# The row of node numbers for the one-hot comparison, read from the PSUM bank of running counts

## The chip, the core and the metric

The kernel runs on one core of a Trainium2 chip. The metric is the device time of one execution in microseconds (us). Five engines work side by side, each through its own queue in order: PE (matrix products, with its weight loads as a row of their own, PEld), DVE (vector operations), ACT (activations and copies), POOL (here almost only the issue of scattered DMAs) and SP (here only DMA issue). SBUF is the working memory. PSUM is the memory that PE writes its results to, in eight banks; DVE and ACT read and write it too.

## The reference

A graph network layer over 12500 nodes with 64 features and 212500 edges that come sorted by their destination `dst`:

```python
h = relu(layernorm(x))
e = silu(concat([h[src], h[dst], edge_weight]) @ eW1 + eb1)   # 129 -> 128, per edge
e = silu(e @ eW2 + eb2)                                       # 128 -> 128, per edge
agg = segment_sum(e, src, num_segments=12500)                 # sum over edges with one source
out = x + silu(concat([h, agg]) @ nW1 + nb1) @ nW2 + nb2      # per node
```

Everything is in 32-bit floating point. The sums go by `src`, while the edges are sorted by `dst`.

## The kernel before

The nodes are dealt to 100 buckets of 125 nodes (`L = 125`, `NB = 100`). The per-node products `h @ eW1` for the source half (`ta`) and the destination half (`tb`) are computed first, a few buckets at a time, and kept in DRAM. Then two kinds of work run interleaved.

**Blocks.** The edges are read in 208 blocks of 1024 in the order given. For a block, `count` finds a row in a bucket-ordered table `q` in DRAM for each edge. DVE compares bucket numbers (`oh`, line 393) and sums them per partition (`each`, line 398). PE adds these sums to the running counts of all buckets with two matmuls onto one PSUM tile named `counts` (lines 413 and 432), which holds 128 x 100 numbers in a bank of its own. DVE reads the counts back (`mine`, line 447; `rank`, line 449) and writes the destinations `to` (line 451), of which four buffers exist. `send` then makes the `tb` part of each edge by PE matmuls (`qp`, line 475), ACT copies it to `qs` (lines 484 and 485), and POOL scatters 128 edges at a time to `q` (line 488, 1661 scatters). A block is issued in four pieces: `oh` and `each` in the first, the matmul of line 413 in the second, that of line 432 in the third, `mine`, `rank` and `to` in the fourth.

**Steps.** As soon as a rank range of `q` is full ("level", 16 of them), the rows of four buckets at a time are loaded (`qt`, line 559) and worked on in 450 steps of 512 edges. A step consists of `lr` (PE, line 596, spreads each edge's number of the node within the bucket over partitions), `oneT` (DVE, line 601), `pt` (PE, lines 610 and 616, adds the `ta` part), a silu on ACT (line 620), the product with `eW2` (line 648), a silu (line 652), `one` (DVE, line 629) and `seg` (PE, line 662). `one` is a 0/1 matrix of 128 edges x 125 nodes for each of four tiles: it is 1 where the edge's node number equals the column's number. It compares `nodes1`, a row 1 to 125 in SBUF, the same on all partitions, with the edge's number in `qt`. `seg` multiplies it with the edges' values and so sums them per node; `aggT` (DVE, line 673) adds the sums of a batch to those so far.

The order on PE, DVE, ACT and SP is written out by hand. The loop at line 1072 goes through the list `turn` (line 681) for each step: `s_pt` of the next step, `s_add`, `s_one_t` two steps ahead, `s_bias`, `s_p2`, `s_one`, `s_seg` of the step before, `s_lr` three steps ahead. At its four `None` places, which are after `s_one_t`, `s_one`, `s_seg` and `s_lr`, pieces of blocks are put in, so many that the table's levels are full when the steps need them. Semaphore waits between engines are put in by the framework from what each instruction reads and writes.

After the last scatter the remaining steps run, and the node part (`nodes`, line 279) writes the output.

Of the kernel before, what the change touches and what calls it, by code (L numbers as in the profile page):

```python
# [28 lines left out]
F32 = mybir.dt.float32  # L29
# [9 lines left out]
P = 128  # L39
L = 125  # L40
# [34 lines left out]
def tile_gnn(ctx: ExitStack, tc: tile.TileContext, x, src, dst, ew, eW1, eb1, eW2, eb2, nW1, nb1, nW2, nb2, out):  # L75
    nc = tc.nc
# [4 lines left out]
    NB = N // L  # L81
# [55 lines left out]
    nodes_i = const.tile([P, L], I32, name="nodes_i")  # L137
# [5 lines left out]
    nodes1 = const.tile([P, L], F32, name="nodes1")  # L143
# [164 lines left out]
    with ExitStack() as work:  # L308
        mm = work.enter_context(tc.tile_pool(name="mm", bufs=4, space=PSUM))
        p2p = work.enter_context(tc.tile_pool(name="p2", bufs=2, space=PSUM))  # L310
        sgp = work.enter_context(tc.tile_pool(name="sg", bufs=1, space=PSUM))
# [2 lines left out]
                engines={mybir.EngineType.PE, mybir.EngineType.DVE, mybir.EngineType.Activation, mybir.EngineType.SP}  # L314
            )
        )
        full = sgp.tile([P, NB], F32, name="counts")
        nc.tensor.matmul(full, before, identb[:, :NB], start=True, stop=True)
        nc.vector.memset(full, -1.0)
        mine = cnt.tile(twos, F32, name="mine")  # L320
        sums = []
        blk, lists = {}, {}
# [262 lines left out]
        def of(k):  # L585

            c, B, n, g = steps[k]
            return batch[c, B], [((g * G + t) % n * G + (g * G + t) // n, (g * G + t) // n) for t in range(G)]
# [34 lines left out]
        def s_one(k):  # L623
            (qt, _, _), tiles = of(k)
            c, B, n, g = steps[k]
            wide = [P, G // n, n, L]
            loc = qt[:, : G * n, H : H + 1].rearrange("p (j b) w -> p b j w", b=G)
            one = wk.tile([P, G, L], F32, name="one")
            nc.vector.tensor_tensor(  # L629
                one.rearrange("p (b j) l -> p b j l", j=n),  # L630
                nodes1[:, None, None, :].to_broadcast(wide),
                loc[:, tiles[0][1] : tiles[0][1] + G // n].to_broadcast(wide),
                op=OP.is_equal,
            )
            st[k]["one"] = one
            if g == n - 1:
                fetch(c * (NB // G) + B + NQ)
# [26 lines left out]
        def s_add(k):  # L664
# [14 lines left out]

        turn = [  # L680
            (s_pt, 1), (s_add, -2), (s_one_t, 2), None, (s_bias, 1), (s_p2, 0), (s_one, 0), None, (s_seg, -1), None, (s_lr, 3), None,
        ]
        hooks = sum(1 for s in turn if s is None)
# [559 lines left out]
```

## Time and profile before

| | |
|---|---|
| median of 3 runs | 2368.57 us (2365.8 to 2370.33) |
| profiled execution | 2374.24 us, its span 2372.4 us |
| PE busy | 2103.3 us (89%), mean granted clock 0.962 |
| DVE busy | 1857.0 us (78%) |
| ACT busy | 1180.9 us (50%) |
| POOL busy | 1697.3 us (72%) |
| scatters, line 488 | 1661, mean 1005 ns |
| `one`, line 629 | 450, mean 673 ns |

How to read the rows that follow. A group row has line, engine, operation, output `<-` inputs by the program's names, shapes and count; behind the bar stand busy time in us and the mean of one in ns, then the idle time of the engine just before these instructions with what ended most of it. A timeline row has start in us, duration in us, engine, line, operation, operands; in brackets the engine's idle time before it and what released it. A row of waits has who waited `<-` for whom, us in total, times, and the longest where a third number stands. A row of a stretch has its bounds and length, then the busy us (with the number of instructions) of PE, PEld, DVE, ACT and POOL, the granted clock, the DMA share and GB/s.

### The profile page before, as it was taken

The numbers are of one execution on the slowest core, as the hardware profiler recorded it, in microseconds if no ns is written. First come the engines' busy times: TensorE is split into PE (matmuls) and PEld (weight loads), VectorE is DVE, ScalarE is ACT, GpSimd is POOL, SyncE is SP. The second block draws the span as 40 slices with busy tenths as digits, with TensorE's granted clock in tenths as the row PEclk, the third lists the DMA queues.
The fourth block names the chain that finished last, engine by engine and source line by source line (L and its number), as shares of the span: only waits on it lengthen the run. The fifth ranks groups of instructions, "written<-read, shape, count | busy, mean of one in ns | idle before, by whom it ended". The sixth has DMA issues, their size and how long they took to land.

```text
span 2372.4 us, 49836 instructions
## 1 busy us (share of the span) xinstructions
PE 2103.3 (89%) x17399; PEld 1847.2 (78%) x17399; DVE 1857.0 (78%) x3291; ACT 1180.9 (50%) x3262; POOL 1697.3 (72%) x1711
## 2 busy tenths in 40 slices
PE   3685888789999999998999889999989999999998
PEld 2452667678888888887788778888878888889998
DVE  7985667678888888787888788878788888788665
ACT  3463554445555555554445445545455555555543
POOL 5677777777777777777777777777777777777310
PEclk9975899899999999999999999999999999999999
DMA  4475676555555555555555555555654444444564
GB/s 136 156 251 194 218 242 190 166 185 174 178 180 173 170 177 176 173 170 157 170 164 172 168 162 172 164 167 170 190 165 131 134 135 135 137 135 141 160 214 122
DMA packets 241429, 401.83 MB, mean 169 GB/s; under 512 B 47528, under 2 KB 140195, under 8 KB 240965
## 3 DMA queue, kind: packets, MB, share of 16 engines
q1 hardware_dynamic: 149411, 216.21, 30.7%
q0 software_dynamic: 53568, 123.20, 14.5%
q10 hardware_dynamic: 38192, 59.17, 8.8%
q8 instruction: 139, 2.28, 0.4%
q14 instruction: 119, 0.97, 0.1%
HBM read 191.09 MB, written 207.01 MB: 168 GB/s over the span
## 4 chain that ended last, share of the span: by engine, by line
PE 50%; DMA 22%; DVE 11%; POOL 6%; issue 6%; ACT 4%; DVEq 0%; SPq 0%; ACTq 0%; POOLq 0%
DMA q<-qs,to 16%; PE seg L662 11%; PE pt L616 10%; PE p L648 8%; POOL q L488 6%; PE qp L475 6%; DMA qt<-q 6%; PE pt L610 6%; PE lr L596 3%; DVE aggT L673 2%; DVE each L398 1%; PE ab L215 1%; ACT e L620 1%; PE z L286 1%; PE o L295 1%
## 5 line engine op out<-in xcount | busy, mean ns | idle before, releaser
L488 POOL DMA_INDIRECT q<-qs,to x1661 | 1669.2, 1005 | 542.5 <-issue 306.1
L620 ACT ACTIVATE e<-pt 128x512 f32<-128x512 f32 x450 | 268.9, 597 | 765.5 <-PE pt L616 704.3
L662 PE MATMUL seg<-one,e 128*128 128x125 f32 x3600 | 505.0, 284 | 106.1 <-DVE aggT L673 89.4
L662 PEld LDWEIGHTS seg<-one,e 128*128 128x128 f32 x3600 | 445.9, 195 | 144.3 <-DVE aggT L673 72.8
L648 PE MATMUL p<-w,e 128*128 128x128 f32 x3600 | 486.1, 278 | 0.0
L648 PEld LDWEIGHTS p<-w,e 128*128 128x128 f32 x3600 | 441.9, 192 | 12.5 <-issue 10.5
L484 ACT COPY qs<-qp 128x256 f32<-128x256 f32 x831 | 309.2, 372 | 266.6 <-PE qp L475 261.4
L601 DVE TENSOR_SCALAR oneT<-lr,part 125x512 f32<-125x512 f32 x450 | 335.1, 745 | 19.2 <-PE lr L596 12.8
L673 DVE TENSOR_TENSOR aggT<-aggT,seg 128x500 f32<-128x500 f32 x425 | 284.4, 669 | 64.6 <-PE seg L662 61.2
L475 PE MATMUL qp<-win,pick 64*128 64x256 f32 x1662 | 319.3, 452 | 17.0 <-ACT qs L484 5.9
L629 DVE TENSOR_TENSOR one<-nodes,qt 128x500 f32<-128x500 f32 x450 | 302.7, 673 | 0.0
L610 PE MATMUL pt<-ident,qt 128*128 128x128 f32 x1800 | 286.1, 283 | 1.4 <-ACT zn L267 0.9
L652 ACT ACTIVATE e<-p 128x512 f32<-128x512 f32 x450 | 269.6, 599 | 30.2 <-PE p L648 18.9
L642 ACT COPY p<-b2f 128x512 f32<-128x512 f32 x450 | 267.6, 595 | 0.0
L616 PE MATMUL pt<-oneT,al 125*128 125x128 f32 x1952 | 262.2, 278 | 0.0
L451 DVE SCALAR_TENSOR_TENSOR to<-rank,offE 128x8 int32<-128x8 f32 x208 | 36.6, 176 | 286.7 <-DMA q<-qs,to 282.1
L616 PEld LDWEIGHTS pt<-oneT,al 125*128 125x128 f32 x1952 | 242.2, 195 | 0.0
L447 DVE TENSOR_TENSOR mine<-oh,counts 128x800 f32<-128x800 bf16 x208 | 204.0, 981 | 39.8 <-PE counts L432 39.5
L596 PE MATMUL lr<-identb,qt 128*125 128x128 bf16 x1800 | 186.9, 228 | 49.6 <-DMA qt<-q 49.1
L610 PEld LDWEIGHTS pt<-ident,qt 128*128 128x128 f32 x1800 | 196.5, 145 | 27.2 <-issue 22.9
L596 PEld LDWEIGHTS <-qt 128*125 128x125 bf16 x1800 | 156.9, 141 | 76.3 <-DMA qt<-q 63.7
L449 DVE TENSOR_REDUCE rank<-mine 128x8 f32<-128x800 f32 x208 | 205.1, 986 | 7.2
(176 smaller groups left out, 1945.7 us busy)
## 6 DMA issues: line engine op xcount, KB each, us to landing
qt<-q SPq DMA_DIRECT2D x450, 288.0 KB
q<-zeros ACTq DMA_DIRECT2D x70, 720.0 KB
q<-qs,to POOLq DMA_INDIRECT x1661
bc<-dests SPq DMA_DIRECT2D x103, 128.0 KB
win<-tb SPq DMA_DIRECT2D x416, 30.0 KB
tb<-got SPq DMA_DIRECT2D x25, 256.0 KB
zd<-zn SPq DMA_DIRECT2D x25, 250.0 KB
zh<-zd SPq DMA_DIRECT2D x25, 250.0 KB
```

The lines of the kernel that those rows point to most:

```text
L475: nc.tensor.matmul(qps[i_][:, :m], pick[half, t * P : (t + 1) * P], win[half, :m], start=True, stop=True)
L484: nc.scalar.copy(qs[:, :m, :H], qp[:, :m, :])
L488: ins = nc.gpsimd.indirect_dma_start(out=q[:], out_offset=bass.IndirectOffsetOnAxis(ap=to[:k, j : j + 1], axis=0), in_=qs[:k, a, :], in_of ...
L596: nc.tensor.matmul(lr[:L, t, :], loc[:, at : at + 1].to_broadcast([P, L]), identb, start=True, stop=True)
L601: nc.vector.tensor_scalar(oneT, st[k].pop("lr")[:L], part1[:L, :], None, op0=OP.is_equal)
L610: nc.tensor.matmul(pt[:, t, :], qt[:, j, :H], ident, is_transpose=True, start=t == 0, stop=False, skip_group_check=True)
L616: nc.tensor.matmul(pt[:, cols, :], a[:L, b, :], oneT[:, cols, :], start=False, stop=True, skip_group_check=True)
L620: nc.scalar.activation(e1, pt, AF.Silu)
L629: nc.vector.tensor_tensor(one.rearrange("p (b j) l -> p b j l", j=n), nodes1[:, None, None, :].to_broadcast(wide), loc[:, tiles[0][1] : ti ...
L648: nc.tensor.matmul(p2[:, t, :], e1[:, t, :], w2, start=False, stop=t == G - 1, skip_group_check=True)
L662: nc.tensor.matmul(item[2][:, b, :], e2[:, t, :], one[:, t, :], start=j < G, stop=j >= G * (n - 1))
L673: nc.vector.tensor_tensor(v, v, seg, op=OP.add)
```

## The change

The tile `counts` grows from 100 to 225 columns of its PSUM bank. The first 100 (`full`) are the counts as before. The 125 behind them (`nodes_p`) receive the row of node numbers by one DVE copy before the blocks begin. In each step `one` reads its first operand from there and no longer from `nodes1` in SBUF. `nodes1` stays, for its other uses. The second operand, the edges' numbers in `qt`, stays in SBUF.

```diff
-        full = sgp.tile([P, NB], F32, name="counts")
+        bank = sgp.tile([P, NB + L], F32, name="counts")
+        full, nodes_p = bank[:, :NB], bank[:, NB:]
         nc.tensor.matmul(full, before, identb[:, :NB], start=True, stop=True)
         nc.vector.memset(full, -1.0)
+        nc.vector.tensor_copy(nodes_p, nodes_i)
@@ s_one
             one = wk.tile([P, G, L], F32, name="one")
             nc.vector.tensor_tensor(
                 one.rearrange("p (b j) l -> p b j l", j=n),
-                nodes1[:, None, None, :].to_broadcast(wide),
+                nodes_p[:, None, None, :].to_broadcast(wide),
                 loc[:, tiles[0][1] : tiles[0][1] + G // n].to_broadcast(wide),
                 op=OP.is_equal,
             )
```

## The prediction

> **What bounds the kernel now.** I read the page first: busy shares, slices and the costliest groups.
>
> ```profile
> span 2372.4 us, 49836 instructions
> PE 2103.3 (89%) x17399; PEld 1847.2 (78%) x17399; DVE 1857.0 (78%) x3291; ACT 1180.9 (50%) x3262; POOL 1697.3 (72%) x1711
> POOL 5677777777777777777777777777777777777310
> L488 POOL DMA_INDIRECT q<-qs,to x1661 | 1669.2, 1005 | 542.5 <-issue 306.1 <-DMA q<-qs,to 76.2 <-ACT qs L485 62.0
> ```
>
> By busy share PE comes first (89%) and POOL only third (72%). But POOL's digit is a flat 7 from slice 3 to slice 36, as if a pace were set there. Its only work in that stretch is line 488, the scatters of edge rows. Their busy time and the idle time ahead of them make 1669.2 + 542.5 = 2211.7 us, which is the time up to the last scatter. So the second view is POOL's timeline, and the third the waits.
>
> ```profile
> 1105.19 0.96 POOL L488 DMA_INDIRECT q<-qs,to  x1 [0.30 <-DMA q<-qs,to]
> 1106.46 0.96 POOL L488 DMA_INDIRECT q<-qs,to  x1 [0.31 <-issue]
> 1107.72 0.96 POOL L488 DMA_INDIRECT q<-qs,to  x1 [0.30 <-issue]
> ...
> 2204.62 0.96 POOL L488 DMA_INDIRECT q<-qs,to  x1 [2.18 <-ACT qs L485]
> ...
> 2221.28 0.96 POOL L488 DMA_INDIRECT q<-qs,to  x1 [0.31 <-issue]
> ```
>
> ```profile
> DVE to L451 <- DMA q<-qs,to: 282.1, 123, 6.8
> ```
>
> From 100 us to 2204 us every scatter follows the one before by the same 0.30 to 0.31 us, whatever the row names as releaser: that is its issue, not starvation. Gaps that are really waits stand only before 100 us and behind 2204 us. The other side of it is DVE's wait: 123 times, 282.1 us in all, `to` (the destinations of a block) could not be written because scatters had not yet freed a buffer. So POOL sets the pace at 0.96 + 0.31 us a scatter. PE, DVE and ACT have 282.1 us of waiting on POOL to give away. After the last scatter some 150 us of other steps follow, which stay as they are.
>
> **Which scatters are slow.** The median scatter takes 0.96 us, the mean 1.005. POOL's and DVE's timelines side by side show where the rest comes from.
>
> ```profile
> 277.69 0.67 DVE L629 TENSOR_TENSOR one<-nodes,qt 128x500 f32<-128x500 f32 x1
> 277.82 1.37 POOL L488 DMA_INDIRECT q<-qs,to  x1 [0.30 <-DMA q<-qs,to]
> ...
> 1007.41 0.67 DVE L673 TENSOR_TENSOR aggT<-aggT,seg 128x500 f32<-128x500 f32 x1
> 1007.59 0.96 POOL L488 DMA_INDIRECT q<-qs,to  x1 [0.30 <-ACT qs L485]
> ...
> 2219.44 0.67 DVE L629 TENSOR_TENSOR one<-nodes,qt 128x500 f32<-128x500 f32 x1
> 2219.81 1.16 POOL L488 DMA_INDIRECT q<-qs,to  x1 [3.92 <-ACT qs L485]
> ```
>
> A scatter that starts while `one` (line 629, the step's one-hot comparison) runs does not get on until `one` ends. In the first pair `one` ends at 278.36 and the scatter at 279.19, 0.83 us later; in others that lose over 60 ns the median is 0.834 us. The middle pair is the same kind of operation, as long, but with one operand in PSUM (`seg`): the scatter takes its 0.96. Of the 1661 scatters 203 start inside a `one` (the first at 246.85, the last the one shown at 2219.81); their mean is 1178 ns. The 173 that start inside `aggT` have a mean of 960.
>
> **The change, part by part.** It removes no instruction. The 450 `one` read the node numbers from PSUM instead of SBUF; a copy of 128x125 into PSUM is added at the start; and `one` now shares a PSUM bank with the counts that PE accumulates.
>
> ```profile
> L629 DVE TENSOR_TENSOR one<-nodes,qt 128x500 f32<-128x500 f32 x450 | 302.7, 673 | 0.0
> L673 DVE TENSOR_TENSOR aggT<-aggT,seg 128x500 f32<-128x500 f32 x425 | 284.4, 669 | 64.6 <-PE seg L662 61.2 <-PE p L648 2.6
> L413 PE MATMUL counts<-each,rest 128*128 128x100 bf16 x208 | 46.3, 222 | 2.2 <-DVE mine L447 2.2
> L432 PE MATMUL counts<-each,before 128*128 128x100 bf16 x208 | 44.8, 215 | 29.2 <-DVE each L398 24.9 <-DVE u L424 3.1 <-DVE counts L430 1.1
> 2.29 0.50 DVE L144 CAST nodes<-nodes_i 128x125 f32<-128x125 int32 x1
> ```
>
> 1. `one` itself. 673 ns with both operands in SBUF, 669 for `aggT` with one in PSUM, at the same 500 elements. I take 0; by the rows it is between -2 and +2 us of DVE in all, off the path.
>
> 2. The scatters. If `one` with a PSUM operand leaves POOL alone as `aggT` does, the 203 scatters fall from 1178 ns to at best 962: 203 x 0.216 = 43.9 us. They will not all be free, since other DVE work also holds scatters up: the remaining 1458 average (1661 x 1005 - 203 x 1178) / 1458 = 981 ns. With that value the gain is 203 x 0.197 = 40.0 us. I take 40, as freed scatters meet the same neighbours. The ends are 0 (`one` still holds POOL up) and the whole excess of all scatters, 1661 x 0.043 = 71 us.
> The Trainium skill, "SBUF — State Buffer", section "Who interferes with whom", says that a VectorE instruction contends with a GpSimd instruction that reads SBUF when both of its inputs lie there, and not when at most one does. The trace agrees: 1178 ns inside `one`, 960 inside `aggT`.
>
> 3. The shared bank. It adds two kinds of wait: a count matmul (lines 413, 432) may have to wait for the `one` that is issued ahead of it, and a `one` for the count matmul ahead of it. Whether the order is kept by columns or by the whole bank no row shows, so the price is bounded. Below: 0. Above: pairing each count matmul with the last `one` that the loop issues before it, 111 of 369 start before that `one` has ended, by 112.7 us together. The first, the longest and the last of them:
>
> ```profile
> 275.65 0.22 PE L413 MATMUL counts<-each,rest 128*128 128x100 bf16 x1
> 277.69 0.67 DVE L629 TENSOR_TENSOR one<-nodes,qt 128x500 f32<-128x500 f32 x1
> ...
> 1101.57 0.22 PE L413 MATMUL counts<-each,rest 128*128 128x100 bf16 x1
> 1108.06 0.67 DVE L629 TENSOR_TENSOR one<-nodes,qt 128x500 f32<-128x500 f32 x1
> ...
> 2120.92 0.21 PE L432 MATMUL counts<-each,before 128*128 128x100 bf16 x1
> 2120.93 0.68 DVE L629 TENSOR_TENSOR one<-nodes,qt 128x500 f32<-128x500 f32 x1
> ```
>
> The other way round 22 of 450 `one` start before the count matmul ahead of them has ended, by 15.4 us. I take the upper end, 128.1 us. Queued behind a waiting count matmul on PE are the transposes, `p` and `seg` of the next step, and `qp`, the source of the scatters; behind a waiting `one` on DVE are `aggT`, `oneT` and `to`. What hides this is the 282.1 us that these engines stand behind POOL: DVE's stand at `to` is often the reason why `one` is late, so PE waits for the same thing one instruction earlier. By stretches, 100:600, 600:1100, 1100:1600, 1600:2100 and the rest, the waits at `to` are
>
> ```profile
>   DMA q<-qs,to: 93.0, 30
> ...
>   DMA q<-qs,to: 48.2, 29
> ...
>   DMA q<-qs,to: 73.3, 31
> ...
>   DMA q<-qs,to: 61.9, 30
> ...
>   DMA q<-qs,to: 5.7, 3
> ```
>
> against new PE waits of 21.7, 14.8, 43.4, 31.2 and 1.6 us, and a shortening of POOL's own time of at most 6.5, 12.8, 11.0, 11.1 and 2.5. What is left is 65, 21, 19, 20 and 2 us: thin, but positive everywhere. So I cost the waits at 0 on the path. Uncovered, they would cost what exceeds 282.1 - 40 = 242 us in all.
> The Trainium skill, "PSUM — Partial Sum Buffer", section "PSUM bank collisions raise a hardware error", says that two engines must not touch one bank in the same quadrant at once even at different columns, so software has to hold one back. No run here shows a collision. By that rule the upper end is the right one; the sum is the same.
>
> 4. The copy: the nearest row is the cast of the same numbers, 0.50 us. It lies among DVE's setup ahead of the first scatter, so I count it in full: +0.5.
>
> 5. POOL's end. The last scatters wait for `qs` from ACT (2.18 us at 2204.62, 3.92 at 2219.81): there PE is the later one, and some of the gain could be lost. The bound is the 282.1 - 276.4 = 5.7 us of cover at the end, so nothing more than a few us.
>
> Sum: -40.0 + 0 + 0 + 0.5 = -39.5. The profiled execution took 2374.2 us around a span of 2372.4; it would come to 2335. It lies 5.7 above the median of 2368.6, and for the median the same difference gives 2329.
>
> **The rivals.**
> A. PE takes over in part. The window with least slack says how near it is:
>
> ```profile
> 600.00:1100.00 500.00, 476.84 (x4177) 427.87 (x4176) 423.93 (x735) 268.52 (x730) 384.08 (x381) 1.00 0.57 173
> 1100.00:1600.00 500.00, 449.97 (x3800) 398.86 (x3799) 401.85 (x697) 249.09 (x690) 383.79 (x382) 0.97 0.54 167
> ```
>
> PE (third number) is busy for 477 of 500 us in the one and 450 in the other. If drawing PE and DVE together makes the new waits twice as long as counted, 256 us against 242 of cover, 14 us come back: 2343. Up to 2360 is possible if the cover is used unevenly. For it: 95% busy. Against it: those waits largely coincide with idle time that PE has anyway (65 waits of `seg` for `aggT`).
>
> B. Slower: PE and DVE fall into step at the bank. It decides once the new waits exceed 242 + 40 = 282 us, 0.68 us for each of the 416 count matmuls. A late pair was late by 112.7 / 111 = 1.015 us. If all 416 wait that long and the `one` too, 422 + 15 - 242 = 195 us come on top of 2329: about 2524 at worst; half the excess gives some 2427. For it:
>
> ```profile
> DVE mine L447 <- PE counts L432: 39.5, 42, 2.7
> ```
>
> a pair of the same two engines on the same tile, which already waits 0.94 us in each of 42 times. Against it: 258 of the 369 find `one` finished.
>
> C. The change frees nothing. Every row with a PSUM operand that overlaps scatters (`aggT`, and `mine` of line 447) has it as the second operand; in the new `one` PSUM comes first and SBUF second. If the place of the operand decides, scatters stay at 1005 ns: 2369, the bank's waits being covered. Only against it: `oneT`, with PSUM first and a scalar from SBUF, has a mean of 980 for scatters that start in it, 962 in the median.
>
> **How the numbers follow.** The forecast 0.66, with a range of its own of 2318 to 2338 (gain 50 to 30). A 0.11, 2338 to 2360. C 0.08, within 0.2% of the old time (4.7 us, about what a measurement here can tell from no change). B 0.15. Faster is the forecast and A, 0.77; same 0.08; slower 0.15. The range takes in the forecast with a lower end where some of the other held-up scatters are freed too, and A and most of C: 2314 to 2366.
>
> **What would show it.** Step 2: the mean of line 488 falls from 1005 to about 980, and scatters that start inside `one` take 0.96. Step 1: `one` stays at 665 to 680 ns. Step 3: new rows of PE's counts waiting for `one`, up to 113 us, while the wait of `to` for scatters falls from 282 to between 100 and 200; POOL's gaps stay at 0.30 until close to the end. It is wrong if POOL shows gaps longer than 0.31 in mid-run with `qs` as releaser (A, B), or if line 488 still has 1005 (C). Also, DVE work that now meets scatters more often than it did could take back some of step 2.

## The result, and the profile after

The changed kernel takes 2333.7 us (median; 2330.2 to 2335.7), the kernel before in the same comparison 2369.5: a ratio of 0.985, with an interval of 0.983 to 0.987. The profiled execution took 2332.1 us around a span of 2330.3, 42 us less than the profiled one before. Two lines were added ahead, so line numbers of the kernel after are two higher: scatters are line 490, `one` 631, `aggT` 675, `to` 453, the count matmuls 415 and 434.

The page of the kernel after, the rows that answer to those shown of before:

```profile
span 2330.3 us, 49976 instructions
PE 2091.2 (90%) x17399; PEld 1842.1 (79%) x17399; DVE 1864.6 (80%) x3292; ACT 1180.1 (51%) x3262; POOL 1649.9 (71%) x1711
POOL 5677777777777777777777777777777777777210
L490 POOL DMA_INDIRECT q<-qs,to x1661 | 1621.8, 976 | 546.2 <-issue 316.8
```

POOL's row of digits is as flat as before. Its scatters are shorter by 47.4 us (1669.2 to 1621.8) and the idle time before them is 3.7 us longer (542.5 to 546.2), so the last scatter ends 43.8 us earlier (2222.2 to 2178.5 us). What follows it is 1.7 us longer, which leaves the 42.1 us by which the span shrank. So the gain came through POOL, with little gained or lost elsewhere. The timeline of POOL and DVE in the kernel after shows a scatter inside a `one`:

```profile
1061.57 0.67 DVE L631 TENSOR_TENSOR one<-counts,qt 128x500 f32<-128x500 f32 x1
1061.79 0.96 POOL L490 DMA_INDIRECT q<-qs,to  x1 [0.31 <-DVE oneT L603]
1062.31 0.67 DVE L675 TENSOR_TENSOR aggT<-aggT,seg 128x500 f32<-128x500 f32 x1
```

Before, a scatter that started so early in a `one` took about 1.3 us; now it takes its 0.96. Of the scatters, 229 start inside a `one`, and their mean is 974 ns (203 with 1178 before). It is not 958, the median of all, because 11 of them start in the last 54 ns of a `one`, when `oh` or `eq` has begun behind it, and are held by that one (1041 to 1366 ns).

The waits of the kernel after (who waited, for whom, us in all, times, the longest):

```profile
DVE to L453 <- DMA q<-qs,to: 163.8, 85, 6.1
PE counts L415 <- DVE one L631: 54.1, 52, 3.0
DVE one L631 <- PE counts L434: 14.3, 19, 3.7
DVE one L631 <- PE counts L415: 10.9, 14, 1.8
PE counts L434 <- DVE one L631: 9.2, 16, 2.4
```

The bank's waits are there although counts and node numbers lie in different columns: 63.3 us of PE and 25.2 us of DVE, 88.5 in all. DVE's standing at `to` fell from 282.1 to 163.8 us, by 118. That is about as much as the shorter scatters (some 42 us) and most of the new waits together; that it paid for them is what the experiments test. On PE the new waits largely stand in the place of older ones. `seg` waits for `aggT` much less, first before, then after:

```profile
PE seg L662 <- DVE aggT L673: 89.4, 65, 6.2
```

```profile
PE seg L664 <- DVE aggT L675: 24.1, 25, 2.6
```

With the first `aggT` of each batch (lines 671 and 673) it is 97.1 to 31.0 us, a fall of 66.1 against the 63.3 us that are new. The time in which PE and PEld both stand idle did not grow: 257 us before, 225 after.

### The profile page after: what moved, and what is told of

The parts are those of the page before. It is cut to its first block, busy times and chain, and to the rows that moved or that the text cites. A ratio compares the mean times of both kernels' runs of the same rounds, so it can differ in the third digit from the quotient of the medians.

```text
span 2330.3 us, 49976 instructions
## 1 busy us (share of the span) xinstructions
PE 2091.2 (90%) x17399; PEld 1842.1 (79%) x17399; DVE 1864.6 (80%) x3292; ACT 1180.1 (51%) x3262; POOL 1649.9 (71%) x1711
## 4 chain that ended last, share of the span: by engine, by line
PE 47%; DMA 20%; DVE 18%; issue 6%; POOL 5%; ACT 3%; SPq 1%; DVEq 0%; ACTq 0%; POOLq 0%
DMA q<-qs,to 14%; PE seg L664 10%; PE pt L618 10%; PE p L650 8%; DMA qt<-q 5%; PE pt L612 5%; PE qp L477 5%; POOL q L490 5%; PE lr L598 3%; DVE one L631 3%; DVE oneT L603 2%; DVE aggT L675 2%; DVE each L400 2%; DVE oh L395 1%; PE ab L215 1%
## 5 line engine op out<-in xcount | busy, mean ns | idle before, releaser
L490 POOL DMA_INDIRECT q<-qs,to x1661 | 1621.8, 976 | 546.2 <-issue 316.8
L664 PE MATMUL seg<-one,e 128*128 128x125 f32 x3600 | 496.4, 281 | 34.2 <-DVE aggT L675 24.1
L664 PEld LDWEIGHTS seg<-one,e 128*128 128x128 f32 x3600 | 440.7, 193 | 106.8 <-issue 35.2
L631 DVE TENSOR_TENSOR one<-counts,qt 128x500 f32<-128x500 f32 x450 | 300.9, 669 | 25.6 <-PE counts L434 14.3
L400 DVE TENSOR_REDUCE each<-oh 128x100 bf16<-128x800 bf16 x208 | 205.1, 986 | 7.1
```

The lines of the kernel that those rows point to most:

```text
L490: ins = nc.gpsimd.indirect_dma_start(out=q[:], out_offset=bass.IndirectOffsetOnAxis(ap=to[:k, j : j + 1], axis=0), in_=qs[:k, a, :], in_of ...
L631: nc.vector.tensor_tensor(one.rearrange("p (b j) l -> p b j l", j=n), nodes_p[:, None, None, :].to_broadcast(wide), loc[:, tiles[0][1] : t ...
L664: nc.tensor.matmul(item[2][:, b, :], e2[:, t, :], one[:, t, :], start=j < G, stop=j >= G * (n - 1))
```

## The experiments

Two theories. P: POOL's scatters set the pace, `one` held them up because both its tensors lay in SBUF, and the bank's waits cost nothing as long as DVE stands at `to` anyway. W: the bank's waits cost what they show, and the relief is larger than the gain by that much; or something else than the relief of POOL made the gain.

In e1 to e4, on one chip, the kernel before took 2374.3 us beside them; in e5 to e8, on another, 2372.0.

### The waits without the relief, and a control

```diff
# e1_waits_alone, on the kernel before
-        full = sgp.tile([P, NB], F32, name="counts")
+        bank = sgp.tile([P, NB + 1], F32, name="counts")
+        full, zero_p = bank[:, :NB], bank[:, NB:]
...
+        nc.vector.memset(zero_p, 0.0)
...
-            nc.vector.tensor_tensor(
+            nc.vector.scalar_tensor_tensor(
                 one.rearrange("p (b j) l -> p b j l", j=n),
                 nodes1[:, None, None, :].to_broadcast(wide),
+                zero_p,
                 loc[:, tiles[0][1] : tiles[0][1] + G // n].to_broadcast(wide),
-                op=OP.is_equal,
+                op0=OP.add,
+                op1=OP.is_equal,
             )
# e2_form_alone: the same, with the zero in a tile of its own in SBUF (zero_s)
```

> The comparison keeps both tensors in SBUF and adds a zero that is read as a scalar from a column behind the counts, in their PSUM bank: the bank's waits without the relief of POOL. Theory P (POOL's scatters set the pace, the waits are covered by DVE's standing at `to`): 2369 us within 0.4%, scatters at 1005 ns as before, some 50 to 90 us of new waits between the counts and `one`, and the wait of `to` for scatters falls from 282 to about 200. Rival W (the waits cost what they show, and the relief had to pay for them): 2369 plus 60 to 90 us, about 2430 to 2460.

> The control of the run before: the same added zero, read from SBUF, so neither waits nor relief. Both theories: 2369 us within 0.3%, `one` at 665 to 690 ns, scatters at 1005 ns, no wait between the counts and `one`. If it is off 2369 by more, the form of the instruction and not the bank explains a part of the run before.

Measured: e1 2381.9 us, ratio 1.003 (1.0015 to 1.0046); e2 2386.2 us, ratio 1.0055 (1.0037 to 1.0073). Rows of groups of e1, then its waits:

```profile
L490 POOL DMA_INDIRECT q<-qs,to x1661 | 1676.0, 1009 | 542.3 <-issue 315.4 <-DMA q<-qs,to 69.5 <-ACT qs L487 63.8
L631 DVE SCALAR_TENSOR_TENSOR one<-nodes,counts,qt 128x500 f32<-128x500 f32 x450 | 331.4, 736 | 20.7 <-PE counts L434 14.1 <-PE counts L415 6.0
```

```profile
DVE to L453 <- DMA q<-qs,to: 203.7, 104, 6.2
PE counts L415 <- DVE one L631: 72.9, 67, 4.8
PE counts L434 <- DVE one L631: 16.1, 25, 3.1
```

and the same two groups and the wait at `to` of e2:

```profile
L490 POOL DMA_INDIRECT q<-qs,to x1661 | 1681.2, 1012 | 542.3 <-issue 317.2 <-DMA q<-qs,to 64.3 <-ACT qs L487 58.4
L631 DVE SCALAR_TENSOR_TENSOR one<-nodes,zero_s,qt 128x500 f32<-128x500 f32 x450 | 328.8, 731 | 0.0
```

```profile
DVE to L453 <- DMA q<-qs,to: 278.4, 117, 5.9
```

e1 has 72.9 + 16.1 + 20.1 = 109 us of waits at the bank that e2 lacks, and is not slower than e2. The wait at `to` is smaller by 75 us (278 against 204), and that of `seg` for `aggT` by 62 (109.0 against 47.1). So while POOL sets the pace the waits alone cost nothing, and the rival's 60 to 90 us are refuted. The 7.7 us by which e1 is above the kernel before, with scatters at 1009 ns instead of the 1005 expected, are close to the 6.8 us by which its scatters' busy time grew.

e2 missed both theories' 2369 and tells more than a control should. Its `one` takes 731 ns instead of 673 and nothing waits for that: DVE stands at `to` for 278 us as before. Yet the time rises by 12 us. The scatters' row has the reason: 1012 ns instead of 1005, which is 12.0 us of busy time (1681.2 - 1669.2). A longer `one` holds scatters longer: 224 start inside it with a mean of 1221 ns, and what they lose against the median rose from 43.9 to 58.1 us. POOL's loss is the kernel's.

### The relief without the waits

```diff
# e3_three_banks_own
-        mm = work.enter_context(tc.tile_pool(name="mm", bufs=4, space=PSUM))
+        mm = work.enter_context(tc.tile_pool(name="mm", bufs=3, space=PSUM))
...
+        nodes_p = sgp.tile([P, L], F32, name="nodes_p")
...
+        nc.vector.tensor_copy(nodes_p, nodes_i)
...
-                nodes1[:, None, None, :].to_broadcast(wide),
+                nodes_p[:, None, None, :].to_broadcast(wide),
# e4_three_banks: the first pair of lines alone
```

> The row of node numbers in a PSUM bank of its own (the pool mm gives one of its four banks away): the relief without the bank's waits. Beside the next run, which has three banks and the row in SBUF. Theory P: 36 to 44 us faster than the next run, if that one is still paced by scatters, the same gain as with the shared bank; scatters inside `one` at about 960 ns. Rival W: 60 us or more faster than the next run, as nothing is paid for waits.

> The kernel before with three instead of four banks in the pool mm. If three banks are enough while scatters set the pace, 2369 us within 0.5%; if products then wait for banks, more, up to some 2450. Only the difference to the run before counts.

Measured: e3 2360.4 us, e4 2395.0, so the relief is worth 34.5 us here, a little under the 36 to 44 expected. That is about what the shared bank gave (35.8), though `one` and the counts do not wait for each other in e3. The granted clock was 0.99 in both, against 0.95 to 0.97 of the kernel before beside them, so they are compared with each other alone. The scatters' groups of e3 and of e4:

```profile
L490 POOL DMA_INDIRECT q<-qs,to x1661 | 1624.3, 978 | 573.7 <-issue 321.4 <-ACT qs L487 90.6 <-DMA q<-qs,to 60.0
```

```profile
L488 POOL DMA_INDIRECT q<-qs,to x1661 | 1672.5, 1007 | 557.0 <-issue 320.2 <-ACT qs L485 70.0 <-DMA q<-qs,to 50.0
```

Scatters got 48.2 us shorter, but POOL's idle time rose by 16.7 us. In e3, 32 gaps of POOL between 600 and 1100 us are longer than 0.31 us, 21.5 us beyond the usual, 8 gaps with 4.1 us in e4. With three banks the wait at `to` is only 112.6 us in e4 and 55.9 in e3, so PE and DVE run closer to POOL's pace. That part of the relief was lost for this reason fits, but was not tried by itself. So e3 doesn't show a gain of the full 48 us without waits; it says that W's 60 us or more did not appear, on a kernel with less cover.

### The place of the operand

```diff
# e5_swapped, on the kernel after
-                nodes_p[:, None, None, :].to_broadcast(wide),
                 loc[:, tiles[0][1] : tiles[0][1] + G // n].to_broadcast(wide),
+                nodes_p[:, None, None, :].to_broadcast(wide),
```

> The changed kernel with the two operands of the comparison exchanged: the edges' numbers (SBUF) first, the row of node numbers (PSUM) second. Theory P: the place of the operand doesn't matter, 2334 us within 0.4%, scatters that start inside `one` at about 960 ns. Rival (the place decides which port is used): scatters inside `one` change by more than 50 ns on average, and the time with them by 10 us or more.

Measured: 2330.0 us. The 219 scatters that start inside `one` have a mean of 970 ns, against 974 with the other order. Which operand lies in PSUM makes no difference to POOL. As e5 differs from the kernel after in nothing else, it also gives the change once more on a single chip: 42.0 us below the kernel before.

### More buffers for the destinations

```diff
# e6_eight_to on the kernel after, e7_eight_to_before on the kernel before
-    top = ctx.enter_context(tc.tile_pool(name="to", bufs=4))
+    top = ctx.enter_context(tc.tile_pool(name="to", bufs=8))
```

> The changed kernel with eight instead of four buffers for `to`. Theory P: POOL still sets the pace, 2334 us within 0.4%; DVE no longer stands at `to` (164 us before, under 60 now), and since `one` was late because of that, the waits of the counts for `one` fall from 63 us to under 35. Rival (the counts wait for `one` for reasons of their own): these waits stay at 55 us or more.

> The kernel before with eight buffers for `to`. Theory P: 2369 us within 0.4%, as scatters set the pace and not the number of buffers; scatters still at 1005 ns. Rival (the buffers of `to` were the bound): faster by 10 us or more.

Measured: e7 2370.9 us, ratio 0.999 (0.998 to 1.000); e6 2326.2 us, ratio 0.980. The gain between the two is 44.7 us. The bank's waits in e6:

```profile
DVE one L631 <- PE counts L415: 26.7, 30, 1.8
PE counts L415 <- DVE one L631: 15.7, 25, 1.2
DVE one L631 <- PE counts L434: 12.0, 17, 1.9
PE counts L434 <- DVE one L631: 1.7, 4, 0.5
```

With eight buffers no row of `to` waiting for scatters is left in e6 or e7, and in the kernel before that changes nothing: the wait was slack and not the bound. PE's waits for `one` drop from 63.3 to 17.4 us. So most of them had come from DVE standing at `to` with `one` behind it, as was expected (under 35). DVE's waits for the counts rose from 25.2 to 38.7. e6 is 7 us below the kernel after, whose chip is not on record; against e5, on the same chip, it is 3.7 us. That gain lies at the end: POOL's gaps behind 2100 us exceed their usual length by 5.0 us, in e5 by 9.8.

### The same for `oh`

```diff
# e8_oh_too, on the kernel after
-        bank = sgp.tile([P, NB + L], F32, name="counts")
-        full, nodes_p = bank[:, :NB], bank[:, NB:]
+        bank = sgp.tile([P, NB + L + NB // 2], F32, name="counts")
+        full, nodes_p, num_p = bank[:, :NB], bank[:, NB : NB + L], bank[:, NB + L :]
...
+        num_s = cnt.tile([P, NB], BF16, name="num_s")
+        nc.vector.tensor_copy(num_s, nodes1[:, :NB])
+        nc.vector.tensor_copy(num_p.bitcast(I32), num_s.bitcast(I32))
...
-                    flat(oh), flat(numbers), buckets[:, None, :].to_broadcast([P, NB // 2, 2 * TB]), op=OP.is_equal
+                    oh,
+                    in_twos(num_p.bitcast(BF16)),
+                    buckets.rearrange("p (t i) -> p t i", i=2)[:, None].to_broadcast(twos),
+                    op=OP.is_equal,
```

> The changed kernel, with the bucket numbers that `oh` compares also in the counts' bank, as 16-bit numbers. `oh` holds up scatters in the changed kernel, 105 that start in it lose 15.4 us. Theory P: scatters fall from 976 to about 967 ns and the time by up to 15 us, 2319 to 2330, less where DVE's standing at `to` is used up (8.6 us are left between 600 and 1100 us). If `oh` gets longer from PSUM (981 instead of 567 ns) or its new waits pile up: 2340 or more, with gaps of POOL in mid-run.

Measured: 2313.2 us, ratio 0.975 (0.973 to 0.977): 20 us below the kernel after, and 17 below e5, which ran on the same chip. Groups of e8:

```profile
L496 POOL DMA_INDIRECT q<-qs,to x1661 | 1601.6, 964 | 547.2 <-issue 307.4 <-DMA q<-qs,to 74.1 <-ACT qs L493 63.7
L398 DVE TENSOR_TENSOR oh<-counts,bkB 128x800 bf16<-128x800 bf16 x208 | 117.6, 566 | 0.0
```

The scatters got another 20.2 us shorter (1621.8 to 1601.6; 18.7 against e5), and the profiled span got 19.3 us shorter. The 102 scatters that start in `oh` have a mean of 958 ns, against 105 with 1104 in the kernel after. The gain was more than the up to 15 expected, because `pick` too met fewer scatters (37 started in it and lost 3.4 us; 62 and 9.8 in the kernel after), though the edit does not touch it. `oh` kept its length. It is the fastest version measured, better than both kernels.

### Going on, on slower chips

```diff
# e9_oh_pick, on e8_oh_too; plus_p is one more column of the counts' bank
-                    nc.vector.tensor_scalar(lists[p][1], lists[p][0], same, plus, op0=OP.is_equal, op1=OP.add)
+                    nc.vector.scalar_tensor_tensor(lists[p][1], lists[p][0], same, plus_p[:, :, None].to_broadcast([P, 2, QR]), op0=OP.is_equal, op1=OP.add)
# e10_oh_pick_to8 and e12_oh_pick_to8_again: the same with eight buffers for `to`
# e11_change_again: the kernel after, nothing changed
```

> The kernel of e8_oh_too, with `pick` also formed with one operand from the counts' bank (the added scalar as a column there, as the second tensor). In e8_oh_too `pick` still cost 3.4 us of scatter time, in the changed kernel 9.8. Theory P: scatters fall from 964 to about 960 ns, the time from 2313 by 3 to 8 us as long as DVE has waits at `to` to give (131 us). Rival (PE and DVE are used up): 2313 or more, with POOL gaps longer than 0.31 us between 600 and 1100 us.

> The same with eight buffers for `to`, which took 7 us off the changed kernel (from 2334 to 2326), most of it at the last scatters, that waited for `qs`. Theory P: another 4 to 8 us less than the run before, about 2300. Rival (the buffers help only by undoing waits at the bank): more than 8 us less. If PE is the bound by now: no difference.

> The changed kernel itself once more, beside the next run. On a chip like those of e1 to e8 (kernel before at about 2370 us): 2334 us within 0.3%, scatters back to back. On a chip like that of e9 and e10 (kernel before at about 2906 us, POOL with 668 us of gaps, so that scatters don't set the pace): theory P has nothing to gain there and the new waits fall on PE, so 0 to 1.5% slower than the kernel before.

> The kernel of e10 again. On a chip like those of e1 to e8: about 2300 us (2313 of e8_oh_too, less 3 to 8 for `pick` and 4 to 8 for the buffers), scatters at 959 to 962 ns. On a chip like that of e9: 1 to 2% slower than the kernel before, and slower than the run before this one, as it has more waits at the counts' bank.

`pick` holds scatters although only one of its tensors lies in SBUF, beside two scalars from there: in the kernel before the 64 that start in it (line 408) have a mean of 1133 ns. So two tensors in SBUF are not the only form that does it, and `rank`, which also reads one tensor from SBUF, does not (181 scatters, 961 ns). Why they differ was not tested. In its new form `pick` holds none: 45 scatters with 961 ns in e9, 54 with 957 in e12, against 45 with 1087 in e11. That form costs DVE 738 ns instead of 556.

These runs fell on two chips on which the kernel before takes 2906.4 us (e9, e10) and 2959.0 us (e11, e12), 22 to 25% longer than on the others. There everything was slower than before: e9 1.018 (1.014 to 1.022), e10 1.013 (1.010 to 1.017), e12 1.012 (1.010 to 1.015), and the change itself, e11, 1.012 (1.007 to 1.016), 2993.9 us. e12, expected to be slower than e11, is 3 us above it, which the spread of the runs does not tell from nothing. From the page of e11, and its waits:

```profile
L490 POOL DMA_INDIRECT q<-qs,to x1661 | 1612.8, 971 | 1210.1 <-ACT qs L487 531.9 <-issue 421.3 <-ACT qs L486 167.6
L631 DVE TENSOR_TENSOR one<-counts,qt 128x500 f32<-128x500 f32 x450 | 301.9, 671 | 107.1 <-PE qp L477 27.7 <-remote 24.0 <-PE counts L415 13.6
```

```profile
PE counts L415 <- DVE one L631: 50.4, 34, 6.2
PE counts L434 <- DVE one L631: 48.5, 31, 4.5
```

Scatters are as short as elsewhere, but POOL is idle for 1210 us and waits 700 us for `qs`: it no longer sets the pace. No wait of `to` for scatters is left to pay for anything. PE's counts wait 98.9 us for `one`, and the kernel comes out 35 us slower than the one before. That fits the waits falling on the path once the cover is gone, but no trace of the kernel before exists from such a chip, and the waits weren't tried alone there, so it is argued and not shown. What makes these chips slow isn't settled either. Operations of DVE and POOL last as long (`one` 671 ns, scatters 971), but PE's are longer on average (`seg` 294 ns instead of 281, `qp` 476 instead of 453) and keep it busy for 2358.8 us instead of 2091.2, with its clock granted at 0.884 instead of 0.958. PE and PEld stand idle together for 607 us instead of 225. So of the 655 us that the span of e11 is longer than that of the kernel after, 268 are busy time of PE and 382 idle time. ACT and DVE wait 694 us for a releaser that the profile puts outside the core or on an unknown queue (`remote`), where the kernel after has no such wait. What `pick` and the buffers would add to e8 on a chip of the first kind stays open.

## Why the prediction was right

Step by step, for the chips on which the kernel before takes some 2370 us:

- **What bounds the kernel.** Right: e7 (the wait at `to` was slack), e2 and e8 (the time follows the scatters' busy time: 11.9 us for 12.0 in e2, and in e8 a span 19.3 shorter for 20.2).
- **Step 1, `one` itself,** at 0: 673 to 669 ns.
- **Step 2, the scatters,** at -40: 47.4 us of busy time. Starts inside `one` fell to 974 ns. Of the 47.4 us, 6.6 are not the change's: the median of all scatters is 958 ns instead of 962, and it is 962 in all of e1 to e4 and 958 in all of e5 to e8, with relief or without, so it goes with the chip. 40.8 us remain against 40.0. On one chip, e7 and e6 differ by 44.3 us of busy time (1666.3 to 1622.0), and e4 and e3 by 48.2. So the mechanism is right and 40 the right size, but that it fits to 1 us is luck: how many scatters fall into `one`, `oh` and `pick` changes from version to version (229, 219 and 216 into `one` in the kernel after, e5 and e6). The 981 ns taken for freed scatters came out as 974, or 978 at the median of the profile before.
- **Step 3, the bank's waits,** 0 on the path, out of at most 128.1 us: 88.5 us were seen, and 109 alone in e1, without cost. Between 600 and 1100 us 8.6 us of the wait at `to` are left, where 21 were worked out; in the other three long stretches 64.1, 52.3 and 38.7, where 65, 19 and 20 were. The cover held, with little to spare. What the prediction used against rival A, that the waits coincide with idle time PE has anyway (`seg` for `aggT`), is borne out: 66.1 of 97.1 us of it went.
- **Step 4, the copy,** at +0.5: the first scatter starts at 21.2 us instead of 20.8.
- **Step 5, the end,** "a few us": POOL's gaps behind 2100 us cost 11.0 us instead of 8.2.
- **The sum** was -39.5. The profile showed -42.1, the medians -35.8, and e5 beside the kernel before -42.0.

Rival C fell with e5. Rival A appeared in weak form only where a bank of PSUM had been taken away (e3). Rival B, at 0.15, did not happen on these chips. On the slow ones the result has its sign (+35 us; B gave +58 at half its excess), but not by its condition: it needed waits above 282 us, whereas e11 shows 117 us of them at the bank (98.9 of PE, 18.4 of DVE) and no cover at all. The prediction took the cover of 242 us for one of the kernel; it belongs to the kernel on a chip like the one it was read on.

## What to carry to other kernels

Where a queue runs back to back, look at the spread of its operations and at what other engines do when the long ones start: here 203 of 1661 scatters carried 44 of 71 us, all behind one kind of vector operation, and neither idle rows nor the waits showed it. Moving one small constant operand to PSUM took that away for `one`, in e8 for `oh` and in e9, in another form of the instruction, for `pick`. New waits on engines that already stand behind the bound cost nothing up to the size of that standing, so add them up by stretches first; and a gain that leans on such slack may turn round on a chip that has none, as it did on the slow one here, though the cause there is argued and not shown.

## What was not expected of the hardware

- `oh`, 800 16-bit elements, takes 566 ns with one operand in PSUM and 567 with both in SBUF, less than the 981 ns of `mine`, which has 800 elements, one operand in 32 bits and a 32-bit result. So the operand in PSUM did not make it slower.
- Adding a scalar to `one` cost 58 ns each (673 to 731 ns), although the elements are the same; and that alone made scatters 7 ns longer on average (1005 to 1012).
- The kernel before ran 22 to 25% longer on two chips. In e11, on one of them, operations of DVE and POOL had the same length as elsewhere; PE was busy for 268 us more and idle for 382 us more. A change worth -1.5% on the others was worth +1.2% on the one of these two where it ran.
